# A gated graph and state-space kernel: two rows of per-token numbers go through DRAM instead of TensorE transposes

## The chip, the cores and the metric

The kernel runs on one core of one Trainium2 chip. The metric is the device time of the whole program in microseconds; lower is better. A core has TensorE (PE, with weight loads shown as PEld), VectorE (DVE), ScalarE (ACT), GpSimd (POOL) and SyncE (SP), which issues this kernel's DMAs. Each engine takes its own instructions strictly in order and waits on semaphores for the others.

## What is computed

The input x is 64 batches of 256 tokens with 256 features in float32, and adj is a 256 x 256 mask. Two layers follow each other; a layer is a graph part and a feed-forward part, each with a layer norm ahead of it and a residual after it.

```
x = x + gnn0(layernorm(x), adj)     # relu MLP, dense attention, MLP, masked attention
x = x + ffn0(layernorm(x))          # top-k tokens through a gelu MLP
x = x + gnn1(layernorm(x), adj)     # one masked attention
x = x + ffn1(layernorm(x))          # a Mamba-2 block and a linear layer

# ffn0
weights = x @ wr + br                        # one number a token
sel = the 127 tokens with the greatest weights
y = (gelu(x[sel] @ w1 + b1) @ w2 + b2) * weights[sel]
processed = zeros; processed[sel] = y;  return processed + x

# an attention
e = leaky_relu(f1[:, None] + f2[None, :])    # f1, f2: one number a token each
att = softmax(where(adj > 0, e, -inf));  out = elu(att @ h)
```

What matters below are the two places where a number per token is needed as a row. The tokens of a batch lie on the partitions, 128 at a time, so that a number per token is a column. To rank the tokens by weight, and to add f2 of all tokens to f1 of one, each partition needs the numbers of all 256 tokens of its batch side by side.

## The kernel before

A group is two batches: 512 tokens, four chunks of 128 (C = 4, G = 2). There are 32 groups. Each goes through three lanes: lane a is gnn0 (first_part), lane b is ffn0 and then gnn1 (middle), lane c is ffn1 (last) with the store of the result. The first group's lane a is split into two half-size lanes (a and d), the last group's lane c into two (e and f), and lane w readies the weights at the start. Up to three groups are on the core at a time, one in each lane.

Every lane is a Python generator. A yield ends a step, and the strings FIRST, ORDER and LAST say, letter by letter, which lane takes its next step; FIRST is for the start, ORDER is repeated once a group, and LAST is for the end. The strings come from a planner outside the kernel, and the instructions of each engine are emitted in just that order (tc.manual_schedule). All DMAs of the kernel stand in one queue, SP's, in that order as well.

The row of the weights is made in ffn0: L602 multiplies each chunk by wr and sums along the free axis into one column of wc, L605 adds the bias, and four transposes (tr, L254) of a wc column broadcast to 128 x 128 give wrow, a PSUM tile that has the row on every partition. Two passes on DVE for each chunk (L622, L625) count the tokens that come first, and L628 turns the count into a 0/1 matrix pick. TensorE multiplies it with the tokens (psel), ACT copies the result out (sel, L641), and the MLP follows (ph, v, g, py, L663 to L674).

The row of the scores is made in the same way in scores, which all three attentions call: four transposes give fb, from which L446 adds the mask and takes the maximum (with no mask, L437 takes the maximum alone), L459 is the leaky ReLU, L463 the exponential with its sum, L468 the reciprocal, and L473 on POOL the division. Then turned transposes the result (pt, L489 copies it to at). The last attention is that of gnn1, where f comes from L715: for s = 1 (f2) first, then for s = 0 (f1).

The tiles come from rotating buffers: all PSUM tiles share 8 banks; in SBUF tag pk has 3 buffers (pick, sel, pT and the two e tiles of gnn1), tag v has 2 (v, y and the at tiles of gnn1). ffn1 already sends rows through DRAM: the running sums csT of each head are written to csd (L786, L787), and spread_row (L809) reads each head's row back to all partitions as a tile E. ffn1 also copies half of a tile to other partitions with a DMA (cs, L874 and L876), which the products pb need.

The rest of ffn1 that the prediction speaks of: after the transposes of its normalized tokens (pt, copied to xT by L419) come the products pd with W_dt, from which DVE and ACT work out the running sum csT (L773 to L781); then pp with W_in, one m after another, each followed by a convolution of four taps (L841 on ACT, three passes L845 on DVE, the tanh L850 on ACT, L851 on DVE). For each head, E is cut off (L820), exponentiated (L826) and multiplied by cb (L899), and py is the product with E; pz gives the gate gz (L907, L908), L924 and L925 combine. At the end pss and pst sum squares, and po (L961) adds the result to xt.

Of the kernel before, what the change touches and what calls it, by code (L numbers as in the profile page):

```python
# [8 lines left out]
F32 = mybir.dt.float32  # L9
I32 = mybir.dt.int32  # L10
BF16 = mybir.dt.bfloat16
AF = mybir.ActivationFunctionType
ALU = mybir.AluOpType
AX = mybir.AxisListType

P = 128
ALPHA = 0.2
# [1 line left out]
GELU_C = 0.7978845608028654  # L19
GELU_A = 0.044715  # L20
FIRST = (
    "dwddadadwaaadawdaaddadaddaaaaadddaaddaaaaddaddaddadaaadaddaddwawdaaaaaaadddadddawdaaaaadadaadaddbaba"
    "aaabaaaabbaawaaaabwaabaaaaababbbaabbbwababababbbbabaaaabaabaawabababbaaaaabbbaaabbbbabbbaababbababab"
    "baababbbaaaabbabbbabbbaaacwccaababcaababbaabcaaabaaabacabbabbbbbaaabaabaabcbcabaabwbbaacabbaabawabca"
    "bbbab"
)
ORDER = (
    "cAaaccbbbbbbacabaccccbccaabacccabcbccabaacbccacabcaaaacacacbcccccbcacabcccbcaaacacbbccccccacaaccbcac"
    "cbacacabccabcccbcbBabccaccbcccabbcacaacbaccacbcbaacbcbbcbcababcbbcbCccbbbbaacaacabcaabbcbbabbbbbccc"
)  # L30
LAST = (
    "ececefefceecbbceccbbcbffbbbccfcbbfceccebbfcccbefccbcbeceebfcccecccecccceccfbccbcecccbccbeeccbefceccf"
    "ccccccfeeebbccecccfecffffcccfbffebcccbfbceffbccbcccefebbcefcccfceeebcbccccbfefccbcccbfbffcbbccccbcbb"
    "cfceefcbfbbcfefcbbcffbfecccbfcbfefbbbfbfbccffeeeebffbeccccfffebbfebbefbecfcbccccccbcbbcbffcccbeeceec"
    "ebfecbbbbcebffcceccbccccbeccebccececbbefcccffecfccffccfecfebcebceeceecebcffbcfeccfffcfecfeccefcececc"
    "cfe"
)


# [1 line left out]
def kernel(ctx: ExitStack, tc: tile.TileContext, a: dict, out: bass.AP):  # L41
# [5 lines left out]
    nc = tc.nc  # L47
    x = a["x"]
    B, N, D = x.shape
# [19 lines left out]
    def psum(name):  # L69
        return ps.tile([P, 512], F32, tag="ps", name=name)  # L70

    def cons(name, *shape, dt=F32):
        return const.tile(list(shape), dt, tag=name, name=name)
# [17 lines left out]
    ident = cons("ident", P, P)  # L91
# [75 lines left out]
    mask1 = cons("mask1", P, 2, N, dt=BF16)  # L167
# [57 lines left out]
    rowd = ctx.enter_context(tc.tile_pool(name="rowd", bufs=2, space=bass.MemoryType.DRAM))  # L225
# [11 lines left out]
    def tiled(pool, shape, tag, name, bufs):  # L237
        return pool.tile(list(shape), F32, tag=tag, name=name, bufs=bufs)

    def t512(tag, name):  # L240
        return tiled(t2, [P, 512], tag, name, BUFS[tag])
# [4 lines left out]
    def sized_sm(tag, n, most, *rest, bufs=4):  # L246

        return sm(tag, P, most, *rest, bufs=bufs)[:, :n]

    def mm(to, lhsT, rhs, start, stop):  # L250
        nc.tensor.matmul(to, lhsT, rhs, start=start, stop=stop)  # L251

    def tr(to, of, eye):
        nc.tensor.transpose(to, of, eye)  # L254


    def tok(c):
        return slice(c * P, (c + 1) * P)
# [10 lines left out]
    def chunk(xn, c):  # L269
        return xn[c // 2][:, c % 2 * D : c % 2 * D + D]  # L270
# [95 lines left out]
    def sized(G, own=None):  # L366
# [16 lines left out]
        T = G * N  # L383
        C = T // P
# [34 lines left out]
                nc.scalar.copy(xT[k][:, :T], pt[:, :T])  # L419
            return xT  # L420

        def scores(f1, f2, mask, strict, tag):

            yield
            fb = psum("fb")
            for c in range(C):
                tr(fb[:, tok(c)], f2(c).to_broadcast([P, P]), ident)  # L430
            halves = [slice(h * N, (h + 1) * N) for h in range(2)]
            es = [t512(tag, "e") for b in range(G)]
            rows = [fb[:, b * N : (b + 1) * N] for b in range(G)]
            top = sized_sm("top", C, 4)
            if mask is None:
                most = sized_sm("most", G, 2)
                nc.vector.tensor_reduce(most, fb[:, :T].rearrange("p (b j) -> p b j", b=G), AX.X, ALU.max)  # L437
                for c in range(C):
                    nc.vector.tensor_scalar(
                        top[:, c : c + 1], most[:, c // 2 : c // 2 + 1], f1(c), -1.0, ALU.add, ALU.mult  # L440
                    )
            else:
                most = sized_sm("topm", C, 4)
                for c in range(C):
                    e = es[c // 2][:, halves[c % 2]]
                    nc.vector.tensor_tensor_reduce(  # L446
                        e, rows[c // 2], mask[:, c % 2, :], 1.0, -3e38, ALU.add, ALU.max, most[:, c : c + 1]
                    )
                for c in range(C):
                    nc.vector.tensor_scalar(  # L450
                        top[:, c : c + 1], most[:, c : c + 1], f1(c), -1.0, ALU.add, ALU.mult
                    )
            yield
            nm = sized_sm("nm", C, 4)
            nc.vector.scalar_tensor_tensor(nm, top, ALPHA, top, ALU.mult, ALU.min)
            den = sized_sm("den", C, 4)
            for c in range(C):
                e = es[c // 2][:, halves[c % 2]]
                nc.scalar.activation(e, rows[c // 2] if mask is None else e, AF.Prelu, bias=f1(c), alpha=ALPHA)  # L459
            yield  # L460
            for c in range(C):
                e = es[c // 2][:, halves[c % 2]]
                nc.scalar.activation(e, e, AF.Exp, bias=nm[:, c : c + 1], accum_out=den[:, c : c + 1])  # L463
            yield
            if strict:

                nc.vector.scalar_tensor_tensor(den, nm, 1e30, den, ALU.is_lt, ALU.mult)
            nc.vector.reciprocal(den, den)  # L468
            if strict:
                nc.vector.scalar_tensor_tensor(den, nm, 1e30, den, ALU.is_lt, ALU.mult)  # L470
            for c in range(C):
                e = es[c // 2][:, halves[c % 2]]
                nc.gpsimd.tensor_scalar(e, e, den[:, c : c + 1], 1.0, ALU.mult, ALU.mult)  # L473
            return es
# [122 lines left out]
        def ffn0(xt, of):  # L597
            xn = yield from layernorm(xt, *of, "xn")
            wc = sized_sm("wc", C, 4)
# [5 lines left out]
            nc.vector.tensor_scalar(wc, wc, br, None, ALU.add)  # L605
            yield

            wrow = psum("wrow")
            for c in range(C):
                tr(wrow[:, tok(c)], wc[:, c : c + 1].to_broadcast([P, P]), ident)  # L610
            rank = sized_sm("rank", C, 4)
            yield

# [1 line left out]
            for c in range(C):  # L615
                b, h = c // 2, c % 2
# [3 lines left out]
                row = wrow[:, b * N : (b + 1) * N]  # L620
# [29 lines left out]
            for m in range(0, KF, 2):  # L650
                yield
                ph = psum("ph")
                v = t512("v", "v")[:, : 2 * S]
                halves = [slice(i * S, (i + 1) * S) for i in range(2)]
# [36 lines left out]
            for b in range(G):  # L691
# [8 lines left out]
                for h in range(2):  # L700
                    c = 2 * b + h
# [5 lines left out]
        def gnn1(xt):  # L707

            xn = yield from layernorm(xt, *moments(xt, 1), "xn")
            f = sized_sm("f", C, 4, 2)  # L710
            junk = t512("g", "junk")
            for s in (1, 0):
                yield
                for c in range(C):
                    nc.vector.scalar_tensor_tensor(  # L715
                        junk[:, :D], chunk(xn, c), 1.0, Wa[:, s, :], ALU.mult, ALU.mult, accum_out=f[:, c, s : s + 1]
                    )
            es = yield from scores(lambda c: f[:, c, 0:1], lambda c: f[:, c, 1:2], mask1, True, "pk")
            at = yield from turned(es, "v")
            ags = []  # L720
            for b in range(G):
                yield

                pa = psum("pa")
                for k in range(KD):
                    for j in range(2):
                        mm(
                            pa[:, k * N : (k + 1) * N],
                            chunk(xn, 2 * b + j)[:, k * P : (k + 1) * P], at[b][:, j * N : (j + 1) * N],
                            start=(j == 0), stop=(j == 1),  # L730
                        )
                ag = t512("g", "ag")
                nc.scalar.copy(ag, pa)
                ags.append(ag)
            for b in range(G):
                yield
                u = psum("u")
                for half in range(2):
                    for k in range(KD):
                        mm(  # L740
                            u[:, half * D : (half + 1) * D],
                            ags[b][:, k * N + half * P : k * N + (half + 1) * P], W_l1[:, k, :],
                            start=(k == 0), stop=(k == KD - 1),
                        )
                w = t512("g", "w")
                nc.scalar.activation(w, u, AF.Exp)
                yield
                nc.vector.tensor_scalar(w, w, 1.0, -1.0, ALU.min, ALU.add)
                nc.vector.scalar_tensor_tensor(w, u, 1.0, w, ALU.mult, ALU.max)
                nc.gpsimd.tensor_tensor(pair(xt, b), w, pair(xt, b), ALU.add)  # L750
# [331 lines left out]
```

## Time and profile before

| what | value |
|---|---|
| time, median of 3 runs | 3656.5 us (3651.49 to 3656.68) |
| the profiled execution's own time | 3653.81 us |
| its span | 3652.1 us |
| mean granted TensorE clock | 0.99 |
| DVE, ACT, POOL busy | 78%, 60%, 31% |
| DMA engines | about 12% of 16 engines for the kernel's queue |
| transposes wrow | 128, median 272 ns each |
| transposes fb of the last attention | 128, median 273 ns each |
| one group in the middle of the span | 109.75 us |

The page of a profile has the busy time of each engine, then the span in 40 slices with a digit for the busy share, then the chain of work that ended last. Further views list instructions in order of time, the busy time in chosen stretches, and who waited for whom. A line of a timeline has the start, the duration, the engine, the source line, the operation, the tiles it writes and reads, the shape, how many equal instructions are merged, and in brackets how long the engine was idle before it and what ended that.

### The profile page before, as it was taken

What the parts mean: (1) busy time and instruction counts of PE and PEld (TensorE: products, weight loads), DVE (VectorE), ACT (ScalarE), POOL (GpSimd) and SP (SyncE); (2) the same over time, 40 slices, a digit from 0 to 9 for tenths busy, and PEclk for the clock granted to TensorE, in tenths of its full rate; (3) what the DMA queues carried; (4) which work ended last, traced back from release to release, by engine and by line L of the source; (5) the groups of instructions that cost most, each with busy time, mean ns of one, the idle gap of its engine ahead of it and who ended that gap; (6) DMA issues with size and microseconds to landing.
All of it is one profiled execution on the core that took longest, in us unless ns stands there. A gap on an engine that the chain in (4) does not pass through costs nothing.

```text
span 3652.1 us, 50662 instructions
## 1 busy us (share of the span) xinstructions
PE 3533.4 (97%) x17004; PEld 2550.6 (70%) x17004; DVE 2842.1 (78%) x7275; ACT 2189.1 (60%) x4942; POOL 1146.8 (31%) x1274
## 2 busy tenths in 40 slices
PE   8999999999999999999999999999999999999876
PEld 6766776776776776776776776776776777776544
DVE  5577778777778777878777878777878777878776
ACT  4565665665665665666665666655666655666544
POOL 2223333323333323333323333323333323333222
PEclk9999999999999999999999999999999999999989
DMA  3011101111101111101111101111101111101111
GB/s 116 1 39 43 49 15 43 48 42 46 49 15 43 48 40 48 49 15 43 48 40 49 48 16 43 49 40 49 44 20 43 48 40 49 41 23 37 43 43 48
DMA packets 90260, 150.89 MB, mean 41 GB/s; under 512 B 12304, under 2 KB 57232, under 8 KB 90000
## 3 DMA queue, kind: packets, MB, share of 16 engines
q1 hardware_dynamic: 90000, 147.65, 12.1%
q8 instruction: 135, 2.21, 0.2%
q14 instruction: 125, 1.02, 0.1%
HBM read 125.86 MB, written 17.56 MB: 39 GB/s over the span
## 4 chain that ended last, share of the span: by engine, by line
PE 81%; DVE 12%; ACT 4%; issue 1%; POOL 1%; DMA 1%; SPq 0%; ACTq 0%; POOLq 0%; DVEq 0%
PE pp L251 31%; PE u L251 10%; PE py L251 9%; PE po L251 7%; PE pz L251 6%; PE pt L254 5%; PE ph L251 4%; PE pa L251 3%; PE psel L251 2%; DVE st L393 1%; DVE xt L595 1%; DVE g L674 1%; DVE w L498 1%; DVE g L671 1%; DVE w L594 1%; PE pss L251 1%
## 5 line engine op out<-in xcount | busy, mean ns | idle before, releaser
L251 PE MATMUL pp<-W_fc,o 128*128 128x256 f32 (+1 forms) x2048 | 460.1, 379 | 0.4 <-DVE W_fc L286 0.4
L845 DVE SCALAR_TENSOR_TENSOR xs<-pp,conv_w,xs 128x510 f32<-128x510 f32 (+5 forms) x495 | 359.9, 728 | 93.9 <-ACT xs L841 79.9
L251 PEld LDWEIGHTS pp<-W_fc,o 128*128 128x128 f32 x2048 | 381.9, 189 | 67.8 <-issue 15.9
L826 ACT ACTIVATE E<-E,ncs 128x256 f32<-128x256 f32 (+1 forms) x1024 | 382.0, 449 | 61.0 <-DVE E L820 58.3
L473 POOL TENSOR_SCALAR e<-e,den 128x256 f32<-128x256 f32 x384 | 186.8, 505 | 714.2 <-PE pp L251 350.3
L251 PE MATMUL pp<-xT,W_in 128*128 128x512 f32 (+1 forms) x660 | 303.6, 593 | 0.0
L850 ACT ACTIVATE th<-xs 128x512 f32<-128x512 f32 (+1 forms) x165 | 101.7, 617 | 326.6 <-DVE xs L845 311.4
L925 POOL TENSOR_TENSOR xs<-xs,gz 128x512 f32<-128x512 f32 (+1 forms) x132 | 205.9, 1561 | 203.0 <-DVE xs L924 200.5
L251 PE MATMUL py<-w,g 128*128 128x256 f32 x1024 | 236.2, 383 | 20.7 <-DVE g L674 20.7
L899 DVE TENSOR_TENSOR E<-E,cb 128x768 f32<-128x768 f32 (+1 forms) x264 | 250.5, 964 | 1.1
L705 POOL TENSOR_TENSOR xt<-xn,xt 128x512 f32<-128x512 f32 x64 | 81.3, 1270 | 526.1 <-DVE xn L702 525.9
L251 PE MATMUL pz<-xT,W_in 128*128 128x512 f32 (+1 forms) x528 | 242.8, 583 | 0.0
L567 POOL TENSOR_TENSOR o<-w,o 128x512 f32<-128x512 f32 (+1 forms) x132 | 180.7, 1369 | 197.8 <-DVE w L501 197.8
L251 PE MATMUL ph<-sel,w 128*128 128x256 f32 x1024 | 242.0, 379 | 0.0
L251 PE MATMUL po<-W_ol,xs 128*128 128x256 f32 x1024 | 241.3, 379 | 0.0
L251 PEld LDWEIGHTS py<-w,g 128*128 128x128 f32 x1024 | 190.0, 190 | 70.9 <-DVE g L674 46.7
L251 PE MATMUL pp<-xT,mlp_w 128*128 128x512 f32 (+1 forms) x528 | 236.5, 583 | 0.7 <-ACT xT L419 0.7
L251 PE MATMUL u<-at,h 128*128 128x256 f32 x1024 | 236.8, 379 | 0.0
L251 PE MATMUL pp<-o,mlp_w 128*128 128x512 f32 (+1 forms) x528 | 231.1, 590 | 2.9 <-POOL o L567 2.9
L820 DVE TENSOR_TENSOR E<-E,ccs 128x512 f32<-128x512 f32 (+1 forms) x264 | 224.3, 863 | 0.0
L393 DVE BATCH_NORM_STATS2 st<-xt 128x6 f32<-128x256 f32 x512 | 185.1, 413 | 49.7 <-POOL xt L750 23.4
L251 PEld LDWEIGHTS u<-at,h 128*128 128x128 f32 x1024 | 191.7, 190 | 37.6 <-issue 7.3
(179 smaller groups left out, 7722.3 us busy)
## 6 DMA issues: line engine op xcount, KB each, us to landing
E<-csd SPq DMA_DIRECT2D x248, 384.0 KB
xt<-in_x_dram SPq DMA_DIRECT2D x31, 512.0 KB
out_dram<-xt SPq DMA_DIRECT2D x31, 512.0 KB
cs<-xs SPq DMA_DIRECT2D x64, 64.0 KB
E<-csd SPq DMA_DIRECT2D x16, 192.0 KB
w<-in_L_ffn_w_dram SPq DMA_DIRECT2D x2, 1024.0 KB
W_in<-in_L_ffn_W_in_dram SPq DMA_DIRECT2D x1, 1160.0 KB
mlp_w<-in_L_gnn_mlp_w_dram SPq DMA_DIRECT2D x2, 512.0 KB
```

The source lines that it names most:

```text
L251: nc.tensor.matmul(to, lhsT, rhs, start=start, stop=stop)
L254: nc.tensor.transpose(to, of, eye)
L393: nc.vector.bn_stats(st[:, c, :], xt[:, c, :])
L473: nc.gpsimd.tensor_scalar(e, e, den[:, c : c + 1], 1.0, ALU.mult, ALU.mult)
L567: nc.gpsimd.tensor_tensor(o1[m], w, o1[m], ALU.add)
L705: nc.gpsimd.tensor_tensor(pair(xt, b), xn[b], pair(xt, b), ALU.add)
L820: nc.vector.tensor_tensor(diag, diag, ccs[:, :, :, h : h + 1].to_broadcast([P, G, 2, P]), ALU.min)
L826: nc.scalar.activation(e[:, b, to], e[:, b, to], AF.Exp, bias=ncs[:, b, half, h : h + 1])
L845: nc.vector.scalar_tensor_tensor(s3[:, :, d:], p3[:, :, : N - d], conv_w[:, m, 3 - d : 4 - d], s3[:, :, d:], ALU.mult, ALU.add)
L850: nc.scalar.activation(th, s, AF.Tanh)
L899: nc.vector.tensor_tensor(e2, e2, cb2, ALU.mult)
L925: nc.gpsimd.tensor_tensor(yt, yt, gz, ALU.mult)
```

## The change

Two functions are touched, and one is added. as_row writes the four columns of a number per token into a row of 512 numbers in DRAM with one DMA; the read side takes the row to all 128 partitions. In ffn0 wrow becomes an SBUF tile (tag v) that one DMA fills from that row. In gnn1 the row of f2 is written as soon as the four passes for s = 1 are emitted, and scores gets it as an argument: four DMAs of 128 x 256 put it straight into the e tiles, and the masked maximum then reads and writes the same tile. The two attentions of gnn0 keep their transposes. The three strings of the order are new.

```diff
--- before.py
+++ after.py
@@ -19,21 +19,21 @@
...
 ORDER = (
-    "cAaaccbbbbbbacabaccccbccaabacccabcbccabaacbccacabcaaaacacacbcccccbcacabcccbcaaacacbbccccccacaaccbcac"
...
+    "Acaccbbabbbcabacccccacbaabbcbacccbaacaacbbccacabcaaaaaacbccaccccaccbcbcccabacaaccbcbacccccccaaccbacc"
...
@@ -419,18 +419,31 @@
                 nc.scalar.copy(xT[k][:, :T], pt[:, :T])
             return xT
 
-        def scores(f1, f2, mask, strict, tag):
-
-
-
-
-            yield
-            fb = psum("fb")
-            for c in range(C):
-                tr(fb[:, tok(c)], f2(c).to_broadcast([P, P]), ident)
+        def as_row(columns):
+
+            row = rowd.tile([4 * P], F32, tag="row", name="row")[:T]
+            nc.sync.dma_start(row.rearrange("(c p) -> p c", p=P), columns)
+            return row
+
+        def scores(f1, f2, mask, strict, tag, row=None):
+
+
+
+
             halves = [slice(h * N, (h + 1) * N) for h in range(2)]
             es = [t512(tag, "e") for b in range(G)]
-            rows = [fb[:, b * N : (b + 1) * N] for b in range(G)]
+            if row is None:
+                yield
+                fb = psum("fb")
+                for c in range(C):
+                    tr(fb[:, tok(c)], f2(c).to_broadcast([P, P]), ident)
+                rows = [fb[:, c // 2 * N : (c // 2 + 1) * N] for c in range(C)]
+            else:
+                for b in range(G):
+                    for half in halves:
+                        nc.sync.dma_start(es[b][:, half], row[b * N : (b + 1) * N].partition_broadcast(P))
+                yield
+                rows = [es[c // 2][:, halves[c % 2]] for c in range(C)]
             top = sized_sm("top", C, 4)
             if mask is None:
                 most = sized_sm("most", G, 2)
@@ -444,7 +457,7 @@
                 for c in range(C):
                     e = es[c // 2][:, halves[c % 2]]
                     nc.vector.tensor_tensor_reduce(
-                        e, rows[c // 2], mask[:, c % 2, :], 1.0, -3e38, ALU.add, ALU.max, most[:, c : c + 1]
+                        e, rows[c], mask[:, c % 2, :], 1.0, -3e38, ALU.add, ALU.max, most[:, c : c + 1]
                     )
                 for c in range(C):
                     nc.vector.tensor_scalar(
@@ -456,7 +469,7 @@
             den = sized_sm("den", C, 4)
             for c in range(C):
                 e = es[c // 2][:, halves[c % 2]]
-                nc.scalar.activation(e, rows[c // 2] if mask is None else e, AF.Prelu, bias=f1(c), alpha=ALPHA)
+                nc.scalar.activation(e, rows[c] if mask is None else e, AF.Prelu, bias=f1(c), alpha=ALPHA)
             yield
             for c in range(C):
                 e = es[c // 2][:, halves[c % 2]]
@@ -605,9 +618,8 @@
             nc.vector.tensor_scalar(wc, wc, br, None, ALU.add)
             yield
 
-            wrow = psum("wrow")
-            for c in range(C):
-                tr(wrow[:, tok(c)], wc[:, c : c + 1].to_broadcast([P, P]), ident)
+            wrow = t512("v", "wrow")[:, :T]
+            nc.sync.dma_start(wrow, as_row(wc).partition_broadcast(P))
             rank = sized_sm("rank", C, 4)
             yield
 
@@ -715,7 +727,9 @@
                     nc.vector.scalar_tensor_tensor(
                         junk[:, :D], chunk(xn, c), 1.0, Wa[:, s, :], ALU.mult, ALU.mult, accum_out=f[:, c, s : s + 1]
                     )
-            es = yield from scores(lambda c: f[:, c, 0:1], lambda c: f[:, c, 1:2], mask1, True, "pk")
+                if s == 1:
+                    row = as_row(f[:, :, 1])
+            es = yield from scores(lambda c: f[:, c, 0:1], lambda c: f[:, c, 1:2], mask1, True, "pk", row)
             at = yield from turned(es, "v")
             ags = []
             for b in range(G):
```

More of the change, by code (lines that the diff above doesn't have):

```diff
@@ L21 @@
 FIRST = (
[L22 to L25, printed above, removed]
+    "wdddaaaadwaadddaaddadadaadaaddwaadddadddadaaadaadadadaaadadaddaawawaaadadddaddddaaaaadaadaddaadaaaba"
+    "baawbaaaabbabaaaaaabawbbabaaabaaaababbbaabbbbaababaabaababwaawbbabbbaaaaababaabbaaabbbbabbbabbabaabb"
+    "aabaaababawwbbabbababbbabacacaabbbcaaaaababccbaaaaababbaacbaabacabbbbawabacabwabbbbaabaaacaabbbbaabb"
+    "cbbab"
 )
 ORDER = (
-    "cAaaccbbbbbbacabaccccbccaabacccabcbccabaacbccacabcaaaacacacbcccccbcacabcccbcaaacacbbccccccacaaccbcac"
-    "cbacacabccabcccbcbBabccaccbcccabbcacaacbaccacbcbaacbcbbcbcababcbbcbCccbbbbaacaacabcaabbcbbabbbbbccc"
+    "Acaccbbabbbcabacccccacbaabbcbacccbaacaacbbccacabcaaaaaacbccaccccaccbcbcccabacaaccbcbacccccccaaccbacc"
+    "ccacaccbabcabccccbaabBbbccbccaccccaabacbacccccbabbbbacbccabbbbccCacacbbbbbaaaaccbacbbabacbabbbbcccb"
 )
 LAST = (
[L32 to L36, printed above, removed]
+    "ffefcbeccfbcbefeeccbfbffccbfcbcbecccbebcbcebcfbfeffccccfcfcccbfccceeececfeffcbfbecfeccfcbccbcccccbff"
+    "ecccefcffecfbfbcbfbeceefcccccecbbcbceccbfffbccbccefeccfccfbfcefcbcefcbececcccfcbfcceecccefcbbecefebc"
+    "bcebcececbbbbcecefcbeebcbecbbcbccbebcbbcfccbebbfcfcffbcbbccffeebecebefcccbebcbecbcbcbfbeccccbfbbcbcc"
+    "ceccbcfbffccffbbcfeccccfeceeeebfcefbffeccccfebecfecbbcccbeccbcccfecccfeeceffecbffcececccceefceecfcfc"
+    "ccf"
 )
```

## The prediction

> **What bounds the kernel now.** I read the page's busy row, clock row and chain first, then one steady period.
>
> ```profile
> PE 3533.4 (97%) x17004; PEld 2550.6 (70%) x17004; DVE 2842.1 (78%) x7275; ACT 2189.1 (60%) x4942; POOL 1146.8 (31%) x1274
> PE   8999999999999999999999999999999999999876
> PEclk9999999999999999999999999999999999999989
> PE 81%; DVE 12%; ACT 4%; issue 1%; POOL 1%; DMA 1%; SPq 0%; ACTq 0%; POOLq 0%; DVEq 0%
> ```
>
> PE is busy in 97% of the span at full clock, and is 81% of the chain; only the last 250 us are looser. The order repeats every 109.75 us (one group; 30 of them make the middle), so I read the table of windows and PE's waits for one period.
>
> ```profile
> 1649.20:1758.95 109.75, 108.80 (x531) 78.64 (x529) 87.46 (x224) 67.82 (x154) 35.79 (x39) 1.00 0.12 41
> ```
> ```profile
> PE py L251 <- DVE g L674: 0.6, 1, 0.6
> PE pst L254 <- ACT ss L944: 0.2, 1, 0.2
> PE pd L251 <- ACT xT L419: 0.2, 1, 0.2
> ```
>
> A wait of PE is listed from the modelled end of the matmul before it, which is some 0.27 later than the time at which the next could have issued; with that the three cost about 0.8, 0.4 and 0.3 us. DVE (87.46 of 109.75) has 22 us of slack in a period, ACT 42, DMA 88%. So PE time is the metric, and a wait elsewhere counts only where PE meets it.
>
> **What the skill says.** "TensorE: Matmul & The Clock Gate", Part 4 (PE-mode transpose), gives about 275 ns for a 128x128 transpose in a kernel's context. The trace agrees on the duration (272 ns median), but in a row they follow at a quarter of it, and that is what counts here:
>
> ```profile
> 1687.26 0.60 PE L254 MATMUL fb<-ident,f 128*128 128x128 f32 x4
> 1687.70 1.47 PE L254 MATMUL pt<-ident,xs 128*128 128x128 f32 x12
> ...
> 1726.73 0.60 PE L254 MATMUL wrow<-ident,wc 128*128 128x128 f32 x4
> 1727.17 2.78 PE L251 MATMUL pp<-W_hand,o 128*128 128x258 f32 x12
> ```
>
> Four take 0.44 us from start to the next instruction. "DMA: Bandwidth & Descriptors", Two DMAs through the same engine are not ordered, says that a DMA reading what another wrote must be issued after the first one's semaphore: SP stands still for the write. Its Rules for kernel authors say that a strided last dimension takes one descriptor per element: 512 here. No trace before shows such a write. "Perfetto Trace Analysis", Optimizing Scalar/DVE Operations, has about 60 ns of overhead for DVE on SBUF and 125 on PSUM; here the same operation takes 422 ns from SBUF (L602) and 479 with a PSUM row (L622), so it agrees.
>
> **The change, part by part.**
>
> (1) Transposes off PE. 2 sets of 4 per group, 0.44 us each, both back to back with PE work: -0.87 us a period, 32 groups: -28 us. This is the whole gain.
>
> (2) DVE reads rows from SBUF: 8 passes at -57 ns, about -0.5 us a period on an engine with slack: nothing.
>
> (3) The round trip. The nearest is csd: four writes, then SP waits, then 384 KB are spread.
>
> ```profile
> 1759.33 0.29 SPq L787 DMA_DIRECT2D csd<-csT  x1
> 1760.62 1.30 SPq L809 DMA_DIRECT2D E<-csd  x3
> ```
>
> From the last write's issue to the first read's issue: 1.29 us. The row has 512 packets of 4 bytes; the trace's 4-byte packets (column loads at the start) took 9 ns, so over 16 engines +0.3. The read: in the end phase the first E (384 KB) was waited for 2.69 us by the chain; 256 KB I put at 2.3. Together some 4 us; bounds 3.5 (a bare write and read) and 7 (strided writes at several times the price).
>
> At the weights: in the changed order DVE does two E products, gz and one xs between wc and the first tie: 2x0.87+0.61+0.66 = 3.0, and waits there for PE's py as well. What remains of the round trip, 0 to 1.5 us, DVE has to spare: from wc to psel PE has about 11.5 us of work, against 4.0 + 4x1.24 (ties and pick) = 9.0. It costs nothing up to a round trip of 6.5; beyond that, 1 us a group each.
>
> At the scores: between f's second column and the first masked maximum DVE has 16 instructions, 7.9 us: covered. But SP is in order: the two cs loads, issued 6 us after the E loads before, now stand behind the row's write and four spreads (1.6 + 4x0.47), and land about 6.3 us after f; PE wants them at pb, about 10 after f. Covered by 3 to 4 us. Behind the weights' row SP has only the store of the result, which waits 47.8 us anyway.
>
> (4) The order. All three strings are new, and the order of each engine in the built program differs throughout. PE's pieces are the same less the 8 transposes, so what differs is which piece meets a wait. I walked one period of the changed order by hand, with durations of the trace before, counting from the end of psel or from the PE piece named:
>
> (a) pt<-e after psel. Before:
>
> ```profile
> 1733.95 1.95 PE L251 MATMUL psel<-pick,xn 128*128 128x128 f32 x16
> 1735.74 0.60 PE L254 MATMUL pt<-ident,pick 128*128 128x128 f32 x4
> 1741.36 1.04 PE L254 MATMUL pt<-ident,e 128*128 128x128 f32 x8
> ```
> ```profile
> 1735.94 0.59 ACT L641 COPY sel<-psel 128x512 f32<-128x512 f32 x1 [1.37 <-PE psel L251]
> 1736.42 0.59 ACT L647 COPY pT<-pt 128x512 f32<-128x512 f32 x1
> 1736.90 0.52 ACT L463 ACTIVATE e<-e,nm 128x256 f32<-128x256 f32 x1
> ...
> 1738.38 0.50 ACT L463 ACTIVATE e<-e,nm 128x256 f32<-128x256 f32 x1
> ```
> ```profile
> 1739.36 1.85 POOL L473 TENSOR_SCALAR e<-e,den 128x256 f32<-128x256 f32 x4 [3.61 <-DVE den L468]
> ```
>
> POOL ended 0.15 us before PE came. In the changed order ACT has, between psel and these exponentials, also the four Prelus (1.6), two v and one square (1.4): they start at 4.2 us after psel's end instead of 1.2, POOL ends at 8.6, and PE, which has pt, ph, po, ph, po (7.35) and four transposes (0.44) in front of the second half, waits 0.9. ph also now follows psel's copy at once. +0.9.
>
> (b) pd: both transposes of xn now stand directly in front of it (0.87 of cover), while ACT does w (0.48) and the copy (0.57) after u: 0.5 lost, before 0.3. +0.15.
>
> (c) py after ph: before 10.56 us from pd's second half to the waiting py; PE now has 9.6 of work there instead of 9.7. +0.1.
>
> (d) pt<-e of the first attention: DVE now does the row maximum before the convolution, so ACT's tanh, which stands ahead of the exponentials, comes later; POOL's first pair is done 7.7 us after fb, PE is there at 7.35 (before: at 9.1). +0.4.
>
> (e) last py: both E products now come behind wc, 9.8 us after u; PE is there after mlp2, pz and half a projection, 9.5. +0.2.
>
> Each is good to about 0.3. Sum +1.75, less 0.87: +0.9 a period, x30 = +27. First and last group lose 1.7 of transposes but have little cover (1.3 us of DVE work at the last weights): +3. In all about +29, on the profiled execution's 3653.8 (span 3652.1 and 1.7 around it) 3683; the median of the runs is 2.7 above it, so I say 3684.
>
> **Rivals.** *Waits that do not appear* (faster): PE before loses so little to waits that an order made in the same way may lose as little; each of my five waits then has cover that I missed, such as ACT or DVE running earlier than I place them. Its place is ACT's order behind psel: (a) alone is half of the sum. From the point where the new waits sum to under 0.87 it is faster; with none, -28 + 3: 3629, with half of them about 3655. For it: 1.7 us of waits in 109.75 now. Against: the order of ACT and PE is fixed, and the durations are the trace's. 3628 to 3648.
>
> *Even*: waits eat just the transposes, 3649 to 3664.
>
> *The round trip decides*: 4-byte writes to DRAM at several times 9 ns; above 6.5 us psel waits, above 8 pb too; at 8 us +1.5 a period more: 3730. Against: 9 ns packets, an idle queue.
>
> That the change does not do what it says is excluded: the built program has 256 transposes fewer, and 64 writes of rows.
>
> **How the numbers follow.** A measurement tells 0.2% (7 us) from no change. Forecast 3665 to 3712 (waits of 1.2 to 2.7 a period): 0.62; waits that do not appear 0.22; even 0.11; round trip 0.05. So slower 0.67, same 0.11, faster 0.22. From 3640 to 3712 some 0.12 below and 0.07 above are left out; the forecast's own range is 3665 to 3712.
>
> **What would show it.** Right: a period of about 110.6 us, with PE waiting for POOL's e about 0.9 us after psel and again after fb; DVE's wait for the row's DMA at tie under 1.5 us; pb without a wait. Wrong: a period near 108.9 with the same three waits as now (first rival), or PE waiting for pick or cs (third). Wrong in size: waits of PE that I did not list, or a chain in the last 250 us grown by more than 5.

## The result, and the profile after

| what | before | after |
|---|---|---|
| time, median of 4 runs | 3655.45 us (3651.49 to 3656.68) | 4295.26 us (4292.58 to 4297.19) |
| span of the profiled execution | 3652.1 us | 4290.9 us |
| granted TensorE clock over the span | 0.99 | 0.92 |
| one group in the middle, mean of four | 109.7 us | 128.8 us |

The ratio of after to before is 1.175, with a 95% interval of 1.173 to 1.177. It is slower, as forecast, but by 640 us and not by 29. One of e1's four runs below took 15634.5 us at a granted clock of 0.22 and is left out of its number. The page of after shows an idle PE and a lower clock all along the middle, and a chain in which DVE has 21% and DMA 16%, where they had 12% and 1%:

```profile
PE 3754.6 (88%) x16748; PEld 2682.8 (63%) x16748; DVE 2909.1 (68%) x7275; ACT 2211.4 (52%) x4942; POOL 1150.2 (27%) x1274
PE   8789888989888989888989888989888989889657
PEclk9899999999999999999999999999999999999878
...
PE 50%; DVE 21%; DMA 16%; ACT 6%; POOL 3%; issue 2%; SPq 1%; DVEq 0%; POOLq 0%; ACTq 0%
```

The busy time of PE has even grown, by 221 us, with 256 instructions fewer: the same products ran at a lower clock. The table of windows for one group of after (length, then busy time of PE, PEld, DVE, ACT and POOL, then clock, DMA share, GB/s), and who made PE wait in it (us in total, times, longest):

```profile
1676.03:1804.98 128.95, 116.12 (x520) 82.95 (x520) 90.09 (x224) 68.59 (x154) 35.83 (x40) 0.93 0.13 41
```
```profile
PE pb L251 <- DMA cs<-xs: 6.3, 1, 6.3
PE psel L251 <- DVE pick L640: 5.4, 4, 3.4
PE pn L254 <- DVE csT L795: 0.5, 1, 0.5
PE pd L251 <- ACT xT L419: 0.4, 1, 0.4
```

This group is 19.2 us longer than the one shown of before. PE is idle for 12.8 us of it instead of 0.9, and busy for 7.3 us more. The two long waits are the ones the third rival named: pb for cs, and psel for pick. What stands behind them is seen in the same group. First the timeline of SP, the queue that issues all DMAs:

```profile
1707.25 0.37 SPq L425 DMA_DIRECT2D row<-f  x1
1716.21 1.77 SPq L444 DMA_DIRECT2D e<-row  x4
1718.02 0.47 SPq L888 DMA_DIRECT2D cs<-xs  x1
1718.53 0.59 SPq L890 DMA_DIRECT2D cs<-xs  x1
...
1760.38 0.37 SPq L425 DMA_DIRECT2D row<-wc  x1
1770.19 0.32 SPq L622 DMA_DIRECT2D wrow<-row  x1
```

then the first reader of each row on DVE:

```profile
1721.06 0.42 DVE L459 CUSTOM_DVE_ANT_0 e<-e,mask 128x256 f32<-128x256 f32 x1 [6.50 <-DMA e<-row]
...
1774.42 0.48 DVE L634 SCALAR_TENSOR_TENSOR tie<-wrow,wc,before 128x256 f32<-128x256 f32 x1 [9.92 <-DMA wrow<-row]
```

From the issue of a row's write to the issue of its read pass 8.96 and 9.81 us, and from there to the first reader 4.85 and 4.23: round trips of 13.8 and 14.0 us, where the prediction had 4. SP stands still for the 9 us, so the cs loads behind it are issued when the row is, 10.8 us after the write.

What PE does right after its wait, in after and then in a kernel of the experiments below (e6) that has the same order and no such wait:

```profile
1723.92 0.76 PE L251 MATMUL pb<-cs,xs 64*128 64x256 f32 x1 [6.32 <-DMA cs<-xs]
...
1725.67 5.82 PE L251 MATMUL u<-at,h 128*128 128x256 f32 x16
```
```profile
1739.95 3.72 PE L251 MATMUL u<-at,h 128*128 128x256 f32 x16
```

The same 16 products take 5.82 us instead of 3.72. The table of windows has the clock around both waits (third number from the right; the next is the DMA share):

```profile
1717.50:1719.70 2.20, 0.10 (x1) 0.00 (x0) 0.00 (x0) 0.28 (x1) 0.00 (x0) 1.00 0.13 35
1719.70:1723.90 4.20, 0.00 (x0) 0.01 (x1) 1.52 (x7) 1.20 (x3) 0.00 (x0) 0.50 0.59 140
1723.90:1729.95 6.05, 6.03 (x18) 5.02 (x19) 5.42 (x17) 3.26 (x11) 0.36 (x1) 0.50 0.01 3
1729.95:1731.50 1.55, 1.55 (x8) 1.37 (x8) 1.38 (x2) 0.79 (x2) 1.55 (x3) 1.00 0.00 0
...
1772.40:1775.80 3.40, 0.00 (x0) 0.00 (x0) 1.30 (x5) 0.00 (x0) 0.00 (x0) 1.00 0.23 74
1775.80:1777.70 1.90, 0.98 (x4) 0.59 (x4) 1.79 (x6) 0.00 (x0) 0.00 (x0) 1.00 0.00 0
1777.70:1784.55 6.85, 5.79 (x20) 4.95 (x21) 4.58 (x23) 2.46 (x6) 1.20 (x2) 0.50 0.00 0
```

So each long wait is paid twice: for its length, and then with some 6 us of work at half the clock. PE's busy time in the two slow windows, 6.03 and 5.79 us, would take half of that at full clock; by this estimate the clock costs 5.9 us a group, most of the 7.3 us of longer busy time. "TensorE: Matmul & The Clock Gate", Part 1 (What's actually happening), has the clock fall to half after an idle window of about 3.4 us and rise after a busy one. The trace agrees on the half and on the rise, but not that a wait must last 3.4 us: at pb the clock fell about 2 us into the wait, and in e9 below it fell after waits listed with at most 1.1 us.

### The profile page after: what moved, and what is told of

Read it like the earlier page. It is cut to its first block, busy times and chain, and to the rows that moved or that the text cites. A ratio compares the mean times of both kernels' runs of the same rounds, so it can differ in the third digit from the quotient of the medians.

```text
span 4290.9 us, 50334 instructions
## 1 busy us (share of the span) xinstructions
PE 3754.6 (88%) x16748; PEld 2682.8 (63%) x16748; DVE 2909.1 (68%) x7275; ACT 2211.4 (52%) x4942; POOL 1150.2 (27%) x1274
## 4 chain that ended last, share of the span: by engine, by line
PE 50%; DVE 21%; DMA 16%; ACT 6%; POOL 3%; issue 2%; SPq 1%; DVEq 0%; POOLq 0%; ACTq 0%
PE pp L251 15%; PE u L251 7%; DMA row<-wc 7%; PE py L251 6%; PE ph L251 4%; PE po L251 4%; DMA wrow<-row 4%; PE pt L254 3%; PE pz L251 3%; DMA cs<-xs 3%; DVE xs L859 3%; DVE xn L405 3%; PE pa L251 2%; PE psel L251 2%; DVE st L393 2%
## 5 line engine op out<-in xcount | busy, mean ns | idle before, releaser
L486 POOL TENSOR_SCALAR e<-e,den 128x256 f32<-128x256 f32 x384 | 230.7, 617 | 919.8 <-DVE den L481 461.8
L251 PE MATMUL u<-at,h 128*128 128x256 f32 x1024 | 298.2, 450 | 0.5 <-ACT at L502 0.5
L251 PE MATMUL psel<-pick,xn 128*128 128x128 f32 x512 | 145.6, 439 | 161.1 <-DVE pick L640 161.1
L634 DVE SCALAR_TENSOR_TENSOR tie<-wrow,wc,before 128x256 f32<-128x256 f32 x128 | 61.5, 480 | 322.1 <-DMA wrow<-row 322.1
L913 DVE TENSOR_TENSOR E<-E,cb 128x768 f32<-128x768 f32 (+1 forms) x264 | 273.3, 1058 | 1.1
L251 PE MATMUL ph<-sel,w 128*128 128x256 f32 x1024 | 270.8, 411 | 0.0
L251 PEld LDWEIGHTS u<-at,h 128*128 128x128 f32 x1024 | 227.3, 230 | 50.3 <-issue 11.9
L653 ACT COPY sel<-psel 128x512 f32<-128x512 f32 x32 | 18.8, 586 | 423.9 <-PE psel L251 423.9
L459 DVE CUSTOM_DVE_ANT_0 e<-e,mask 128x256 f32<-128x256 f32 x128 | 53.0, 425 | 270.6 <-DMA e<-row 269.1
L251 PEld LDWEIGHTS psel<-pick,xn 128*128 128x128 f32 x512 | 112.1, 307 | 197.8 <-DVE pick L640 190.7
```

The costliest lines, as they stand in the source:

```text
L459: nc.vector.tensor_tensor_reduce(e, rows[c], mask[:, c % 2, :], 1.0, -3e38, ALU.add, ALU.max, most[:, c : c + 1])
L634: nc.vector.scalar_tensor_tensor(tie, row, wc[:, c : c + 1], before[:, h, :], ALU.is_equal, ALU.mult)
L913: nc.vector.tensor_tensor(e2, e2, cb2, ALU.mult)
```

## The experiments

Each kernel is compared with new runs of before, whose medians were 3652.9 to 3655.6 us.

**e1: the order alone.** Both sets of transposes are put back; only the strings differ from before.

```diff
-            wrow = t512("v", "wrow")[:, :T]
-            nc.sync.dma_start(wrow, as_row(wc).partition_broadcast(P))
+            wrow = psum("wrow")
+            for c in range(C):
+                tr(wrow[:, tok(c)], wc[:, c : c + 1].to_broadcast([P, P]), ident)
...
-                if s == 1:
-                    row = as_row(f[:, :, 1])
-            es = yield from scores(lambda c: f[:, c, 0:1], lambda c: f[:, c, 1:2], mask1, True, "pk", row)
+            es = yield from scores(lambda c: f[:, c, 0:1], lambda c: f[:, c, 1:2], mask1, True, "pk")
```

> The changed order of pieces, with both sets of transposes kept and no row through DRAM. Step (4) of the prediction, by itself, puts its five new waits at 1.75 us a period: 3655 + 30 x 1.75, some 3708 us. The rival theory, that the order costs nothing and the two rows cost everything, says 3650 to 3662 us, with PE's waits in the middle at about 2 us a period. If the order accounted for a good part of the 640 us, it would be above 3800.

Measured: 3747.0 us (expectations further down reckon with 3750), ratio 1.025 (1.023 to 1.027). Above what step (4) says, far above "the order costs nothing", and far below 640. The longest wait of a group is one that the changed kernel cannot have, PE at the transposes of the row, because this order puts them right behind wc:

```profile
1765.12 0.62 PE L254 MATMUL wrow<-ident,wc 128*128 128x128 f32 x4 [0.85 <-DVE wc L618]
```

So e1 overstates the order; e10 takes that away.

**e2 and e3: one row alone.** The first half of the edit above gives e3 (scores only), the second half e2 (weights only).

> The changed kernel with only the weights' row through DRAM; the scores' row is transposed as before. If the two round trips each hold up PE and add, the wait of the first tie (322 us in the changed kernel) stays and that of the masked maximum (269 us) goes: some 3655 + 340, 3980 to 4010 us. If a longer period only lets one wait hide behind the other (the two share one chain), one row alone would still cost most of the 640 us: above 4150. The prediction's step (3) says that this row costs 0 to 1 us a group: below 3700.

> The changed kernel with only the scores' row through DRAM; the weights' row is transposed as before. If the round trips add: 3655 + 300, 3930 to 3970 us, with the waits at the masked maximum and at pb for the cs loads kept. If one chain holds both, above 4150. The prediction's step (3) says nothing lost: below 3700.

Measured: e2 3978.6 us (ratio 1.089, 1.088 to 1.091), e3 4033.4 us (1.104, 1.102 to 1.106). Over e1 the weights' row costs 232 us, the scores' row 286; with the order's 94 that makes 612 of the 640. So the round trips nearly add, and each by itself costs far more than step (3) allowed. The size of e3 was missed: its range ended 63 us lower. I hadn't counted the slower clock behind the wait at pb: the mean clock is 0.956 over e3's 4028.7 us and 0.988 over e1's 3750.8, which is up to 132 us at full clock, an estimate that would cover it; no run takes it away by itself.

**e5: both rows in the order of before.** The strings of the change are taken back.

> Both rows through DRAM as in the changed kernel, but in the order of pieces of the kernel before. If the changed order costs 97 us and nothing else (order alone: 3750), this gives 4295 - 97, about 4200 us. If the changed order spreads the work around the two rows so that more of the round trip is covered, this order is slower still: above 4300, with waits at the first tie and at the masked maximum longer than 10.1 and 8.4 us a group.

Measured: 4385.5 us (ratio 1.200, 1.198 to 1.202). The second case: DVE waits 395.5 us at the first tie, 12.4 a group, against 10.1 in after, and 8.2 against 8.4 at the masked maximum. The changed order costs something by itself and gives 90 us back once the rows go through DRAM: it puts more work between wc and tie.

**m1 and m2: the write by itself.** Both compute nothing of the reference and copy x to the output. One write and a read that waits for it are issued by SP, three times for each shape. In m1 the first pass ran among other transfers and isn't read; m2 has the order fixed by hand.

```diff
+            t = d(f"near_{i}", 512)
+            trial("near", i, turned(t), cols[:, :4], t[:1].unsqueeze(0))
+            for name, gap in (("apartB8", 2), ("apartB16", 4), ("apartB32", 8), ("apartB64", 16)):
+                t = d(f"{name}_{i}", 512, gap)
+                trial(name, i, turned(t[:, 0]), cols[:, :4], t[:1, :1])
```

> Nothing of the reference is computed: x is copied to the output, and single transfers are measured one after another, each with the next issue on its queue waiting for it. The row's write (512 packets of 4 bytes to neighbouring addresses in DRAM) should take about 9.8 us from issue to the next issue, as in the changed kernel. Theory one, a price per packet: about 1.5 us and 16 ns for each, so 256 packets 5.5, 128 packets 3.5, and 128 packets of 16 bytes 3.5 as well; spread addresses change nothing. Theory two, neighbours: packets that share a piece of DRAM wait for each other, so elements 64 or 512 bytes apart take about 2 us, and 128 packets of 16 bytes still several us. Theory three, a fixed price of any write that is waited for: all of them 8 to 10 us, rows of 512 bytes or 2 KB too. The prediction's step (3) says 1.6 us for the row, and for all others 1.3 to 1.6. Into SBUF, or in reads of 4 bytes, theory two and three say 2 us, theory one 3.5 for 128.

> Nothing of the reference is computed: x is copied to the output, and single writes to DRAM are measured in an order written out by hand, each from its issue to the next issue that waits for it. The first set of single transfers gave 8.3 to 10.7 us for 512 packets of 4 bytes side by side, 6.9 to 7.5 for 128 of them, 2.2 for 512 that lie 64 bytes apart, and 1.4 for 128 of 16 bytes side by side. Theory neighbours: what costs is how many packets fall into the same piece of DRAM, so the time falls step by step with the gap: 8 bytes about 5 us, 16 about 3.5, 32 about 2.7, 64 about 2.2, and pairs of 8 bytes side by side about 4 to 5. Theory smallest packet: a packet of 4 bytes is cheap only if nothing else is near, so 8, 16 and 32 all stay above 6 and the pairs drop to 1.5 to 2. 16 packets of 4 bytes in one piece of 64 bytes: 2 us if it is the number, 6 to 7 if one shared piece is enough. Into SBUF and in reads of 4 bytes: about 2.

Measured, from the issue of the write to the issue of what waits for it:

| write | us |
|---|---|
| 512 packets of 4 bytes side by side (the change's row) | 8.3 to 10.9 |
| 256 of them (m1) | 8.1 to 8.4 |
| 128 of them (m2) | 7.1 to 7.3 |
| 512 of 4 bytes, 8 / 16 / 32 / 64 bytes apart | 3.3 to 4.7 / 2.5 to 2.7 / 2.0 to 2.3 / 1.8 to 2.3 |
| 256 of 8 bytes side by side | 3.4 to 3.8 |
| 128 of 16 bytes side by side | 1.4 to 1.9 |
| 4 of 512 bytes | 1.2 |
| 16 of 4 bytes side by side | 1.3 |
| 128 of 4 bytes into one SBUF partition | 2.0 to 2.1 |
| 512 of 4 bytes read from DRAM | 2.1 to 2.2 |
| the 256 KB read of a row to 128 partitions | 3.1 to 3.3 |

The third pass of m2, for the row, the pairs and the packets of 16 bytes; the difference of two starts is the time:

```profile
132.21 0.39 SPq L35 DMA_DIRECT2D near<-cols  x1
140.68 0.24 SPq L37 DMA_DIRECT2D rd_near<-near  x1
...
160.84 0.36 SPq L35 DMA_DIRECT2D pairs<-cols  x1
164.59 0.23 SPq L37 DMA_DIRECT2D rd_pairs<-pairs  x1
166.08 0.33 SPq L35 DMA_DIRECT2D fours<-cols  x1
167.49 0.23 SPq L37 DMA_DIRECT2D rd_fours<-fours  x1
```

A price per packet falls: 512 packets take 8.5 us side by side and 1.9 when they are 64 bytes apart. A fixed price of a waited write falls too: 512-byte rows take 1.2. So does the theory of the smallest packet, which had all of 8, 16 and 32 bytes apart above 6 us. What costs is many packets of 4 bytes beside each other in DRAM, and nothing of the kind is seen in SBUF or in reads.

**m3: how many, and in which order.** Again nothing of the reference is computed and x is copied. 16 to 128 packets of 4 bytes from a column, and 128 from one partition that fill the same 512 bytes in large or small steps.

```diff
+            for word, n in (("sixteen", 16), ("thirtytwo", 32), ("sixtyfour", 64), ("onetwentyeight", 128)):
+                t = d(f"{word}_{i}", n)
+                trial(word, i, t.unsqueeze(1), cols[:n, :1], t[:1].unsqueeze(0))
```

> Nothing of the reference is computed: x is copied to the output, and single writes to DRAM are measured from issue to the next issue that waits for them. 16 packets of 4 bytes side by side took 1.3 us, 128 of them 7.1 to 7.3. First, 16, 32, 64 and 128: a price for each packet beyond the first 16 says 1.3, 2.2, 3.9, 7.2; a step at some number says flat and then 7. Then 128 packets of 4 bytes from one partition that fill the same 512 bytes, in steps of 256 (2 runs), 64 (8 runs), 32 (16 runs) and 8 bytes (64 runs). If what waits is a packet that follows another into the same small piece, wide steps are cheap (about 2 us) and steps of 8 bytes are dear (above 4); if it is only that many small packets fall into the same 512 bytes, all take about 7.

Measured: 16 packets 1.3 us, 32 3.0 to 3.3, 64 6.8 to 7.1, 128 7.0 to 7.8. The text above has runs and steps the wrong way round: 2 runs go in steps of 8 bytes, 8 in steps of 32, 16 of 64 and 64 of 256. They took 8.9 to 9.4, 7.7 to 7.9, 7.1 to 7.4 and 7.1 to 7.3 us. Even in steps of 256 bytes it is 7, so most of the price isn't that a packet follows its neighbour within the DMA (that adds 2 us at steps of 8 bytes), but that so many fall beside each other. How large the piece is that they share isn't shown: 64 in 256 bytes take 6.8 to 7.1 us here, while the row of m2 with gaps, which has 64 in every 512 bytes, takes 3.3 to 4.7. With the number the time rises up to 64 packets and then slowly: neither the straight line nor one step. What happens in the memory these runs don't say.

**e6: the same change with wider packets.** The order, the reads and the number of DMAs of after stay; the weights' row is written with the four numbers of a partition side by side (16 bytes), the scores' row with the two of a graph side by side (8 bytes). The readers follow: wrow and before are read through a view, f is laid out by s, mask1 is stored in that order once, and the transposes of e step by 2.

```diff
-            nc.sync.dma_start(row.rearrange("(c p) -> p c", p=P), columns)
+            nc.sync.dma_start(row.rearrange("(p c) -> p c", p=P), columns)
...
+            nc.sync.dma_start(
+                row.rearrange("(b p h) -> p b h", p=P, h=2), columns.rearrange("p (b h) -> p b h", h=2)
+            )
...
+            wcols = wrow.rearrange("p (q c) -> p c q", c=C)
...
-                row = wrow[:, b * N : (b + 1) * N]
+                row = wcols[:, 2 * b : 2 * b + 2, :]
```

> The changed kernel, its order and its reads kept; only the layout of the rows in DRAM differs: the weights' row is written as 128 packets of 16 bytes, the scores' row as 256 packets of 8 bytes, and the mask of the last attention, the reads of the row and the transposes of e follow that layout. Measured alone, the writes take 1.4 to 1.9 and 3.4 to 3.8 us instead of 8.3 to 10.9. Theory: the writes of 4-byte neighbours are what the changed kernel loses beyond its order. Then the round trips fall from 14 to about 6 and 8.5 us, the waits at the first tie and at the masked maximum from 10.1 and 8.4 us a group to about 2 and 3, and the time to 3750 (order alone) less 28 for the transposes plus 0 to 60: 3720 to 3780 us. Rival: the round trip as such costs (two waits for semaphores, the 256 KB read of 4.2 us, SP held up): then at most half of the 545 us comes back, above 4000.

Measured: 3760.2 us (ratio 1.030, 1.028 to 1.031), in the range of the theory. SP in one group of e6, and PE's waits in it:

```profile
1728.66 0.37 SPq L434 DMA_DIRECT2D row<-f  x1
1731.95 1.77 SPq L455 DMA_DIRECT2D e<-row  x4
...
1773.55 0.32 SPq L428 DMA_DIRECT2D row<-wc  x1
1775.09 0.32 SPq L634 DMA_DIRECT2D wrow<-row  x1
```
```profile
PE pt L254 <- POOL e L497: 0.6, 2, 0.4
PE pn L254 <- DVE csT L808: 0.5, 1, 0.5
PE pd L251 <- ACT xT L422: 0.4, 1, 0.4
PE ph L251 <- ACT sel L666: 0.2, 1, 0.2
```

The writes take 3.3 and 1.5 us, pb and psel wait for nothing, the clock of the group is 1.00, and 535 of the 640 us are gone. The round trip as such stays, two DMAs and two semaphores for each row, so what cost them is the write of 4-byte neighbours, which the wider packets avoid.

**e7 and e9: wide packets in the order of before.** e7 is e6 with before's strings, e9 has only the weights' row through DRAM, in before's order.

> The same two layouts in the order of pieces of the kernel before. With writes of 4 bytes this order gave 4385 us, with waits of 12.4 us at the first tie and 8.2 at the masked maximum. Writes that are 8 and 5 us shorter leave 4 and 3 us; PE lost about 8.5 us at psel in that run and should lose 0 to 1. Theory: 3655 - 28 + 32 x (0.5 to 2.5), some 3645 to 3705 us, faster than the same layouts in the changed order. Rival (the order is needed once the rows go through DRAM): slower than those, above 3750.

> The kernel before with its own order, and only the weights' row through DRAM, as 128 packets of 16 bytes. Four transposes less are 14 us off; the round trip of about 6 us has 2 us of other DVE work beside it and PE some more. If PE doesn't meet the rest, 3641 us; if it loses 0.5 to 1 us a group, 3655 to 3675.

Measured: e7 3939.2 us (ratio 1.078, 1.075 to 1.080), e9 3849.0 us (1.054, 1.052 to 1.055). Both were missed, and my theory of what this order can hide falls: the rival of e7 was right. In e9 DVE's and PE's waits over the whole run say why:

```profile
DVE tie L641 <- DMA wrow<-row: 142.4, 31, 5.6
```
```profile
PE psel L251 <- DVE pick L647: 103.9, 97, 4.2
```

In before PE has 6.8 us of work between the transposes of wrow and psel (1727.17 to 1733.95), and the ties and picks need 5.0. In e9 a round trip of 6.0 us stands ahead of the ties, and these take 6.4, since the view steps through wrow by 16 bytes (0.67 us a pass instead of 0.48): 12.4 against 6.8. By this estimate 5.6 us of a group are not covered; the 195 us over 32 groups are 6.1. In the trace a part of them is clock: PE waits three times at psel in a group, listed with at most 1.1 us each and 3.1 together, and yet the clock falls to half:

```profile
1705.80:1708.50 2.70, 0.98 (x5) 0.59 (x4) 2.59 (x6) 0.00 (x0) 0.00 (x0) 1.00 0.00 0
1708.50:1715.30 6.80, 5.45 (x20) 4.89 (x21) 4.53 (x22) 3.55 (x9) 1.20 (x2) 0.50 0.00 0
```

**e8: cs ahead of the row.** In after, the cs loads are issued as soon as their source is there.

```diff
                 xs[m] = s
+                if m == KI:
+                    bc = s
+                    cs = columns("c8", "cs")
+                    nc.sync.dma_start(cs[:DS, :N], bc[DS:, :N])
+                    if G == 2:
+                        nc.sync.dma_start(cs[DS:, N:], bc[:DS, N:])
...
-            bc = xs[KI]
-            cs = columns("c8", "cs")
-            nc.sync.dma_start(cs[:DS, :N], bc[DS:, :N])
-            if G == 2:
-                nc.sync.dma_start(cs[DS:, N:], bc[:DS, N:])
```

> The changed kernel with the two cs loads issued as soon as their source is there, which puts them ahead of the scores' row in SP's queue. In the changed kernel PE stands 6.3 us at pb until cs comes, at the same moment at which DVE gets its row. If SP's queue is a cost of its own, PE gains some 2 to 4 us a group: 4295 - 32 x 3, 4165 to 4230 us. If the masked maximum behind the row is what decides, PE only meets the same wait later (at the transposes of e or at the banks that xd sets free): 4270 to 4300.

Measured: 4205.4 us (ratio 1.151, 1.149 to 1.153), 90 us less than after. Being behind the row in SP's queue is a cost of its own, 2.8 us a group. The rest only moves: PE now passes pb and stands at u, until DVE has worked off xd, which stands behind the masked maximum and so behind the row.

```profile
PE u L251 <- DVE xd L885: 4.1, 1, 4.1
```

**e10: the changed order with the weights' row alone, in packets of 16 bytes.** It is e6 with the scores' row by transposes.

> The changed order, the weights' row through DRAM as 128 packets of 16 bytes, the scores' row by transposes. In the run with the order alone PE waited 0.85 us a group for wc in front of the transposes of the row, which the changed kernel doesn't have. If that wait and the transposes are gone and nothing comes in their place: 3750 - 32 x (0.44 + 1.1), some 3700 us, so that the new order by itself costs 1.8 us a period, as step (4) of the prediction summed it. If the round trip of 6 us still costs PE about 1 us a group: 3725 to 3745.

Measured: 3713.1 us (ratio 1.016, 1.014 to 1.018), between the two cases. In the middle a group takes 111.0 us, 1.3 more than before, which is what step (4) gives for it (1.75 less the 0.44 of one set of transposes). The other 19 us are lost in the first and last groups. PE's timeline of a group has no wait at psel, and these (idle time in brackets):

```profile
1453.84 0.33 PE L254 MATMUL pn<-ident,csT 64*128 64x64 f32 x2 [0.50 <-DVE csT L800]
1543.37 1.99 PE L251 MATMUL ph<-sel,w 128*128 128x256 f32 x8 [0.24 <-ACT sel L660]
1558.35 1.11 PE L251 MATMUL pd<-xT,W_dt 128*32 128x256 f32 x8 [0.36 <-ACT xT L419]
```

No version tried beats before. e10 and e6 are the nearest, 58 and 106 us above it.

## Why the prediction was wrong

The 640 us in the terms of the sum, from runs: e10 over before +58 (the order, less one set of transposes), e6 over e10 +47 (the scores' row in pairs, less the other set), after over e6 +535 (4-byte packets).

- **Step (1), transposes off PE**: nothing speaks against the 0.87 us a group; they are gone, and what is lost elsewhere is twenty times as much. In a row they follow each other at 0.11 us, which is 40% of their 272 ns and not a quarter; the sum uses the 0.44 for four and stands.
- **Step (2), DVE reads from SBUF**: the 57 ns a pass did not come: tie took 478 ns (median) with its row in PSUM and 480 in SBUF, the masked maximum 420 and 426. L602, which I had compared with, has another form of operand. Of the 60 and 125 ns of overhead in "Perfetto Trace Analysis", Optimizing Scalar/DVE Operations, these passes show nothing. The passes are 12 a group and not 8: eight of the ranking, four of the masked maximum. It cost nothing, since DVE idles in every group.
- **Step (3), the round trip**: this is the step that failed, in its first term, "The row has 512 packets of 4 bytes; the trace's 4-byte packets (column loads at the start) took 9 ns, so over 16 engines +0.3". The price of a packet was right: after's trace has the 512 packets and 16 semaphore writes of a row within 0.37 us, at 7.6 ns each. But a packet's record is not the time until the write is known to be done: in m2 the 512 packets are recorded within 0.38 us both side by side and 64 bytes apart, and the waiting read was issued 8.5 and 1.8 us after the write. SP could issue the read only 9.0 and 9.8 us after the write, not 1.6. The 9 ns came from loads into SBUF, and a 4-byte load of 512 elements does take only 2.1 us (m2). I had looked at the wrong direction. "DMA: Bandwidth & Descriptors" says in Specifications that transfers under 512 bytes are done as read, modify and write (it gives 512 bytes as the least for full rate, not as a delay), and in Anatomy of one DMA, for DMAs that GpSimd issues, that the semaphore waits for the receipt of the last byte. The runs agree that short packets can be dear, but their delay has no limit at 512 bytes: 16 bytes side by side took 1.4 us, 4 bytes 8.5.
- The second term of (3), the read, was also small: 2.3 expected, 4.2 and 4.9 measured, up to its first reader; for the scores it is four reads of 128 KB, twice what was priced. The view that gave the 2.69 us has 4.25 for a later load of E. The bounds of 3.5 to 7 for the sum left out the truth of 14 by a factor of two; "strided writes at several times the price" was taken as the upper end, with no run or row behind "several".
- **The covers in (3)** were right. psel was said to wait beyond a round trip of 6.5 us, 1 us each: 14.0 gives 7.5, and the trace lists four waits of 5.4 together, which with 0.27 for each, as the prediction counts a wait, are 6.5. pb was said to wait beyond 8: 13.8 gives 5.8, measured 6.3, or 6.6 counted in the same way. In e6 and e10, with 6 us at the weights, psel doesn't wait. The queue behind SP was seen, too (e8).
- **The clock** is in none of the terms. After the two long waits of a group PE works some 6 us at half clock each time: by the estimate above 5.9 us, nearly a third of the group's 19.2.
- **Step (4), the order**: its sum holds in the middle (e10: 1.3 for 1.3), in part by luck, since its terms are mixed. Of (a), the pt<-e after psel stand twice for 0.26 and ph for 0.24, together about the 0.9; (b), pd, 0.36 against 0.19, as said; (c), py after ph, is wrong, the wait of before is gone; (d), 0.4, is there in e6, which like after has no transposes of f in front (0.18 listed, 0.45 with the 0.27), and not in e10, where those give it more cover; (e) doesn't appear; a wait at pn, 0.50, was not listed. The ends cost 19 us, not 3. In the last line of the sum, 3683 and the 2.7 above it would be 3686 and not 3684, which decides nothing.
- **The rivals**: "The round trip decides" came true in mechanism and place, with a chance of 0.05. The evidence against it, "9 ns packets, an idle queue", said nothing about completion. With 14 us instead of 8 its own arithmetic gives 7.5 and 5.8 us of waits; with the 5.9 us of the clock and the 0.9 of steps (1) and (4) that is some 20 a group, against 19.2 measured.

What stays open: why 4-byte neighbours in DRAM are slow. The time grows from 16 to 64 of them and slowly after, falls with the distance, and depends little on the order in which one DMA writes them (7.1 to 9.4 us for 128). Whether the memory or the DMA engines hold them up isn't told apart here.

## What to carry to other kernels

A round trip through DRAM costs what its write takes to be confirmed, and that depends on the width of the packets: measure the very shape, or make the last dimension of the DRAM side 16 bytes, which was enough here, and let the reader follow the layout. Numbers of 4 bytes with gaps of 64 were as fast alone (1.8 to 2.3 us) but weren't tried in the kernel. A wait of several microseconds on PE costs its length and then a slower clock; here 11.7 us of waits brought about 5.9 us more, so price it at one and a half times, and short waits close together as well (e9). And where a bound is a multiple of a price that no trace shows, the chance of the rival behind it is not 0.05.

## What the runs showed of the hardware that was not expected

- 4-byte packets side by side into DRAM: 1.3 us for 16, 3.0 for 32, about 7 for 64 and 128, 8.3 to 10.9 for 512; 64 bytes apart 1.9 for 512. Into SBUF 128 take 2.0, and reading 512 of them 2.1.
- A DMA's packets can be recorded as done within 0.38 us and its semaphore come some 7 us later (the row of m2).
- PE's clock fell to half for 6.8 us after three waits within 5 us, listed with at most 1.1 us each (e9).
- DVE's two-operand pass over 256 numbers took 0.67 us with a step of 16 bytes on one SBUF operand and 0.48 without.
